# A GNN message layer on one core: a new opening order, clears and loads in smaller and larger pieces, and second operands of VectorE in PSUM

## The chip, the cores and the metric

The kernel runs on one core of one Trainium2 chip. The metric is the time of the device in microseconds (us). Five engines matter: PE multiplies matrices, DVE (VectorE) and ACT (ScalarE) work on elements, POOL (GpSimd) here issues the indirect DMAs, SP (SyncE) issues most other DMAs. Each engine takes its own instructions in a fixed order and waits on semaphores for the others.

## The reference, cut to what matters

```python
# x (6250, 128), src and dst (100000,), edge_attr (100000, 128), W (384, 128); dst is sorted
row, col = src, dst
h = concatenate([x[row], x[col], edge_attr], -1) @ W + b
h = (h - mean(h)) * rsqrt(var(h) + 1e-5) * gamma + beta      # over the 128 features
out = segment_sum(relu(h), row, num_segments=6250)
y = x + out
return (y - mean(y)) / sqrt(var(y) + 1e-5)
```

Every edge gets a message from its two nodes and its own features, the messages are normalized, and each node sums the messages of the edges that have it as `src`. The edges come sorted by `dst`, so the sum needs another order.

## The kernel before, in words

The weight matrix is split into three: `xa = x @ W[0]` (with the bias) for the source node, `xb = x @ W[1]` for the target node and `eT @ W[2]` for the edge. Means are taken out of the weights beforehand.

Edges are worked on in 782 tiles of 128, four tiles to a piece; there are 196 pieces, and one call of `edges` handles one of them (a slot). Because `dst` is sorted, a piece needs only 42 neighbouring rows of `xb`: `win` loads that window from the table `xb_d` in DRAM (three bf16 parts), `db` loads the piece's offsets within the window for all partitions (from `drel_d`), DVE makes the one-hot `ohd` from it (L345), and PE adds `eT @ W[2]` (L351) and `ohd @ win` (L352) in the PSUM tile `hp`. ACT copies it to one of eight buffers `hs` (L354) with the local node number beside it (L356), and POOL scatters the rows, one indirect DMA for each tile (L360), to the DRAM table `sorted` of the split, where the edges of one block of nodes stand together.

Where a row goes is worked out by `places` for a group of tiles: a one-hot over the 50 blocks (`oh`, L264), a running count (`sc`, L266, a scan over 50 x T elements), products (`far` L280, `sc` L281), sixteen matmuls (L287), and small instructions that end in `place_i` (L305).

The tiles are in three splits of 260, 260 and 262 tiles, each with its own `sorted` table. While the edges of split s + 1 are scattered, the 50 blocks of split s are worked on: `begin` loads a block (`hl`, L411, 6 x 128 rows), makes the one-hot `ohe` of local node numbers (L415) and transposes it (`tr` L422, `ohn` L423); `middle` adds the gathered `xa` rows to `hl` in PSUM (`sel`, L433 and L437), squares and sums (ACT, L441), and makes `msg` (DVE, L449); `end` sums the messages of each node (`pa`, L457) into `acc`. The blocks of split 2 have no edges beside them. `finish` (L467) handles five blocks' worth of nodes at the very end: residual and layer norm.

Before the first `edges` call stand the set-up of constants and weights, `source_blocks` (block and local number of each source), `windows` (the offsets, written to `drel_d`), thirteen projections `project(g, 1)` that write `xb_d`, and the first group of places. Rows of `sorted` that no edge fills are cleared by three large DMAs on ACT's queue (`clear`, L147). `side` holds the other groups of places, two other small steps, the projections `project(g, 0)` that make `xa`, and the other clears; one of them is given out in every second slot of split 0.

The order on each engine is the work of a scheduler with priorities, from the order of the calls and from buffers; only the opening stands under a higher priority. PSUM has eight banks: two `hp`, one `pa`, two `tr`, three `sel`.

Of the kernel before, what the change touches and what calls it, by code (L numbers as in the profile page):

```python
# [15 lines left out]
P = 128  # L16
# [7 lines left out]
NB, BN = 50, 125  # L24
NPAD = 6400
PT = 4
WN = 42
PIECES = 196
# [3 lines left out]
SPLITS = [(260, 6, 4, [32, 66, 66, 66, 30]), (260, 6, 4, [65] * 4), (262, 6, 4, [66, 66, 66, 64])]  # L32
TMAX = 66
PG = 7
G = 3
# [32 lines left out]
def fast_path(ctx, tc, io, bad_d):  # L68
# [9 lines left out]
    xb_d = dram.tile([3, NPAD, D], BF16, name="xb_d")  # L78
# [10 lines left out]
    proj_pool = early.enter_context(tc.tile_pool(name="proj", bufs=2))  # L89
    src_i = setup.tile([P, TILES], I32, name="src_i")  # L90
    nc.sync.dma_start(src_i, io["srcT"])
    dst_i = setup.tile([HALF, 2, PT * P], I32, name="dst_i")
    nc.sync.dma_start(dst_i, io["dstC"])
    w3 = const.tile([P, 3, D], F32, name="w3")
    nc.scalar.dma_start(w3, io["W"].rearrange("(k p) d -> p k d", p=P))
    base_i = const.tile([1, PIECES], I32, name="base_i")
    nc.scalar.dma_start(base_i, io["base"])
# [3 lines left out]
    for t, v in ((gamma_bc, io["gamma"]), (b_bc, io["b"]), (beta_bc, io["beta"])):  # L101
        nc.scalar.dma_start(t, dram_ap(v, 0, [[0, P], [1, D]]))
# [4 lines left out]
    nc.gpsimd.iota(part_i, pattern=[[1, 1]], base=0, channel_multiplier=1)  # L107
    spare_i = setup.tile([P, TMAX], I32, name="spare_i")
    nc.gpsimd.iota(spare_i, pattern=[[P, TMAX]], base=0, channel_multiplier=1)
    ident = const.tile([P, P], F32, name="ident")  # L110
    make_identity(nc, ident)
    eps = const.tile([P, 1], F32, name="eps")
    nc.vector.memset(eps, LN_EPS)
    iota_row = const.tile([P, P], F32, name="iota_row")
    nc.vector.tensor_copy(iota_row, iota_i)
    iota_h = const.tile([P, NB], BF16, name="iota_h")
    nc.vector.tensor_copy(iota_h, iota_i[:, :NB])
    part = const.tile([P, 1], F32, name="part")
    nc.vector.tensor_copy(part, part_i)
    ones_h = const.tile([P, P], BF16, name="ones_h")  # L120
    nc.vector.memset(ones_h, 1.0)
# [16 lines left out]

    spare_rows = max(k - f for _, k, f, _ in SPLITS)
    empty = const.tile([P, spare_rows, ROW], F32, name="empty")  # L140
# [3 lines left out]
    def clear(s):  # L144
        _, k, f, _ = SPLITS[s]
        per = k - f
        return nc.scalar.dma_start(  # L147
            dram_ap(sorted_d[s], f * P * ROW, [[per * ROW, P], [k * P * ROW, NB], [1, per * ROW]]),
            row_bc(flat(empty[:, :per, :]), NB))
# [4 lines left out]
    nc.vector.tensor_scalar(sgn, gamma_bc, 0.0, 2.0, op0=ALU.is_ge, op1=ALU.mult)  # L154
    nc.vector.tensor_scalar(sgn, sgn, -1.0, None, op0=ALU.add)
    wsum = const.tile([P, 4], F32, name="wsum")
    nc.vector.tensor_reduce(wsum[:, 0:3], w3, axis=AX.X, op=ALU.add)
    nc.vector.tensor_reduce(wsum[:, 3:4], b_bc.unsqueeze(1), axis=AX.X, op=ALU.add)
    wmean = const.tile([P, 4], F32, name="wmean")
    nc.vector.tensor_scalar(wmean, wsum, 1.0 / D, None, op0=ALU.mult)  # L160
    w = const.tile([P, 3, D], F32, name="w")
    for j in (1, 2, 0):
        nc.vector.scalar_tensor_tensor(w[:, j, :], w3[:, j, :], wmean[:, j:j + 1], sgn,
                                       op0=ALU.subtract, op1=ALU.mult)
    bias = const.tile([P, D], F32, name="bias")
    nc.vector.scalar_tensor_tensor(bias, b_bc, wmean[:, 3:4], sgn, op0=ALU.subtract, op1=ALU.mult)
# [7 lines left out]
    def source_blocks(t0, t1):  # L174
# [7 lines left out]
        nc.vector.tensor_copy(bkt_h[:, c], bkt[:, c])  # L182
        if t1 == TILES:
            for p0 in range(LAST, P, 32):
                nc.vector.memset(bkt_h[p0:p0 + 32, TILES - 1:TILES], 99.0)


    bad = const.tile([P, 3], F32, name="bad")
# [23 lines left out]


    xa = tabs.tile([P, NB, 3 * D], BF16, name="xa")
    acc = tabs.tile([P, NB, ACW], F32, name="acc")
    XG = 4
    n_proj = -(-NB // XG)

    def project(g, k):

        t0 = g * XG
        m = min(XG, NB - t0)
        xT = proj_pool.tile([P, XG * P], F32, name="xT", bufs=4)
        nc.sync.dma_start(xT[:, :m * P], io["xT"][:, t0 * P:(t0 + m) * P])
        ps = psum.tile([P, 4, P], F32, name="hp", bufs=2)
        for j in range(m):
            nc.tensor.matmul(ps[:, j, :], xT[:, j * P:(j + 1) * P], w[:, k, :],
                             start=True, stop=True)
        full = ps[:, :m, :]
        if k == 0:  # L230
            o = xa[:, t0:t0 + m, :]
# [3 lines left out]
        else:  # L235
            xb_t = proj_pool.tile([P, XG, 3 * D], BF16, name="xb")
            o = xb_t[:, :m, :]
        nc.scalar.copy(o[:, :, 0:D], full)
        rest_t = proj_pool.tile([P, XG, D], F32, name="rest")
        rest = rest_t[:, :m, :]  # L240
        nc.vector.tensor_tensor(rest, full, o[:, :, 0:D], op=ALU.subtract)
        nc.scalar.copy(o[:, :, D:2 * D], rest)
        nc.vector.tensor_tensor(o[:, :, 2 * D:3 * D], rest, o[:, :, D:2 * D], op=ALU.subtract)
        if k == 1:
            for i in range(3):
                nc.sync.dma_start(
                    dram_ap(xb_d, i * NPAD * D + t0 * D, [[NB * D, P], [D, m], [1, D]]),
                    o[:, :, i * D:(i + 1) * D])
# [7 lines left out]
    def places(s, t0, T):  # L256
        cap = SPLITS[s][1] * P
# [5 lines left out]
            for t in (oh, sc, far)]  # L263
        nc.vector.tensor_tensor(oh_v, row_bc(bkt_h[:, t0:t0 + T], NB), col_bc(iota_h, T),  # L264
                                op=ALU.is_equal)
        nc.vector.tensor_tensor_scan(flat(sc_v), flat(oh_v), flat(oh_v), 0.0,  # L266
# [9 lines left out]
        at = place_pool.tile([P, NB], F32, name="at")  # L276
# [49 lines left out]
    def edges(s, q):  # L326
# [28 lines left out]
        with tc.issue_after(evict.ins):  # L355
            nc.scalar.copy(hs[:, :m, D], sloc[:, t0:t0 + m])  # L356
# [463 lines left out]
```

## Time and profile before

| | before |
|---|---|
| time, median of 3 runs | 1531.3 us (1529.97 to 1536.56) |
| time of the profiled execution | 1529.89 us |
| its span in the profile | 1528.1 us |
| granted TensorE clock, mean of the span | 0.874 |
| PE / DVE / ACT / POOL busy | 1162.9 / 805.0 / 658.8 / 843.7 us |
| DMA packets, bytes, mean rate | 147179, 238.46 MB, 156 GB/s |

The span is the profiled part of one execution; 1.8 us of its time lie around it. Busy time is the sum of the instructions' durations; an engine can be idle for long and still set the end, and a busy one can be off the path. In a row of a group, the numbers after the first bar are busy time and the mean ns of one instruction, those after the second the idle time before them and what ended it. In the slices each digit is the busy share of a fortieth of the span (38.2 us) in tenths.

### The profile page before, as it was taken

How to read it: one execution, taken by the hardware profiler on the slowest of the kernel's cores; microseconds unless marked ns; L12 is line 12 of the kernel's file. 1: busy time of each engine (PE TensorE's matmuls, PEld its weight loads, DVE VectorE, ACT ScalarE, POOL GpSimd, SP SyncE). 2: the span in 40 equal slices, each digit the busy share in tenths (PEclk: the TensorE clock that was granted, in tenths of full speed). 3: DMA queues.
4: the chain of work that ended last, by engine and by line, in shares of the span. 5: the costliest groups of instructions: out<-in, count | busy, mean ns of one | idle time of the engine just before them, and what ended most of it. 6: DMA issues, size and time to landing. Idle time of an engine off the chain costs nothing.

```text
span 1528.1 us, 26702 instructions
## 1 busy us (share of the span) xinstructions
PE 1162.9 (76%) x8886; PEld 948.1 (62%) x8886; DVE 805.0 (53%) x2127; ACT 658.8 (43%) x2706; POOL 843.7 (55%) x804
## 2 busy tenths in 40 slices
PE   2555565564565479999999839999999848888885
PEld 2233444353343348888888728888888637677674
DVE  6999453432313425445544305545545327777766
ACT  0011212121010026766666516666676526666563
POOL 0000787877878877777777777777777720000000
PEclk9687877765667679999999959999999969999998
DMA  9944534443333346766666447676767223333330
GB/s 322 347 106 104 168 127 136 134 143 113 118 127 111 103 139 208 207 204 205 202 201 198 127 143 226 204 217 196 211 198 204 74 91 99 101 101 94 109 92 31
DMA packets 147179, 238.46 MB, mean 156 GB/s; under 512 B 64050, under 2 KB 84291, under 8 KB 147031
## 3 DMA queue, kind: packets, MB, share of 16 engines
q1 hardware_dynamic: 101924, 163.14, 37.4%
q0 software_dynamic: 25024, 52.85, 9.7%
q10 hardware_dynamic: 20082, 20.67, 4.3%
q8 instruction: 72, 1.18, 0.3%
q14 instruction: 77, 0.62, 0.1%
HBM read 155.11 MB, written 81.47 MB: 155 GB/s over the span
## 4 chain that ended last, share of the span: by engine, by line
PE 46%; POOL 16%; DVE 14%; DMA 12%; issue 9%; ACT 2%; SPq 0%; ACTq 0%; POOLq 0%; DVEq 0%
POOL sorted L360 16%; PE pa L457 11%; PE sel L433 11%; DMA sorted<-hs,place_i 10%; PE sel L437 8%; PE hp L351 7%; PE tr L422 6%; DVE sc L266 2%; DVE ohe L415 2%; PE pa L287 2%; PE hp L352 2%; DVE msg L449 1%; DVE far L280 1%; ACT sq L441 1%; DVE y L477 1%
## 5 line engine op out<-in xcount | busy, mean ns | idle before, releaser
L360 POOL DMA_INDIRECT sorted<-hs,place_i x782 | 841.9, 1077 | 392.8 <-issue 192.4
L351 PE MATMUL hp<-w,eT 128*128 128x128 f32 x1564 | 324.1, 333 | 171.6 <-ACT hs L354 164.8
L351 PEld LDWEIGHTS hp<-w,eT 128*128 128x128 f32 x1564 | 273.7, 219 | 217.0 <-ACT hs L354 189.9
L354 ACT COPY hs<-hp 128x512 f32<-128x512 f32 x196 | 114.7, 585 | 508.3 <-DMA sorted<-hs,place_i 353.0
L441 ACT ACTIVATE sq<-sel 128x128 f32<-128x128 f32 x900 | 251.7, 280 | 128.0 <-PE sel L437 101.8
L433 PE MATMUL sel<-hl,ident 128*128 128x384 f32 x600 | 260.6, 517 | 24.6 <-DVE frstd L484 15.2
L449 DVE SCALAR_TENSOR_TENSOR msg<-sel,rstd,cut 128x128 f32<-128x128 f32 x900 | 247.4, 342 | 1.5
L457 PE MATMUL pa<-msg,ohe 128*128 128x130 f32 x1800 | 244.7, 282 | 2.4 <-DVE msg L449 1.3
L437 PEld LDWEIGHTS <-ohn 128*128 128x128 bf16 x2700 | 182.2, 98 | 92.5 <-issue 58.2
L457 PEld LDWEIGHTS pa<-msg,ohe 128*128 128x128 f32 x1800 | 220.3, 192 | 8.3 <-DVE msg L449 4.8
L437 PE MATMUL sel<-xa,ohn 128*128 128x128 bf16 x2700 | 211.0, 220 | 0.0
L352 PE MATMUL hp<-win,ohd 126*128 126x128 bf16 x782 | 186.0, 239 | 26.0 <-DVE ohd L345 24.4
L441 ACT ACTIVATION_READ_ACCUMULATOR sq<-sel 128x1 f32 x900 | 176.7, 196 | 0.0
L415 DVE TENSOR_TENSOR ohe<-hl,iota_row 128x768 f32<-128x768 f32 x150 | 140.7, 939 | 66.3 <-DMA hl<-sorted 66.3
L423 ACT CAST ohn<-tr 128x384 bf16<-128x384 f32 x300 | 129.3, 482 | 76.0 <-PE tr L422 73.8
L422 PE MATMUL tr<-ident,ohe 128*128 128x128 f32 x900 | 127.7, 279 | 40.5 <-DVE bad_t L565 27.3
L345 DVE TENSOR_SCALAR ohd<-db,part_w 128x512 bf16<-128x512 bf16 x196 | 67.9, 358 | 161.3 <-PE hp L352 141.1
L422 PEld LDWEIGHTS tr<-ident,ohe 128*128 128x128 f32 x900 | 102.0, 144 | 59.1 <-DVE bad_t L565 27.4
L446 DVE RECIPROCAL rstd<-std 128x6 f32<-128x6 f32 x150 | 28.2, 188 | 194.6 <-ACT std L444 193.4
L433 PEld LDWEIGHTS sel<-hl,ident 128*128 128x128 f32 x600 | 92.4, 194 | 29.3 <-issue 17.1
L352 PEld LDWEIGHTS <-ohd 126*128 126x128 bf16 x782 | 85.8, 110 | 28.4 <-DVE ohd L345 25.8
L287 PE MATMUL pa<-far,ident 128*128 128x462 f32 (+4 forms) x208 | 94.6, 593 | 6.9 <-DVE far L280 6.0
(116 smaller groups left out, 692.6 us busy)
## 6 DMA issues: line engine op xcount, KB each, us to landing
hl<-sorted SPq DMA_DIRECT2D x150, 396.0 KB
eT<-in_eT SPq DMA_DIRECT2D x97, 512.0 KB
db<-drel_d SPq DMA_DIRECT2D x98, 256.0 KB
sorted<-empty ACTq DMA_DIRECT2D x3, 6600.0 KB
sorted<-hs,place_i POOLq DMA_INDIRECT x782
win<-xb_d SPq DMA_DIRECT2D x196, 31.5 KB
xT<-in_xT SPq DMA_DIRECT2D x24, 256.0 KB
xb_d<-xb SPq DMA_DIRECT2D x36, 128.0 KB
```

The costliest lines, as they stand in the source:

```text
L287: nc.tensor.matmul(sums[:, :g * T], wt, flat(v[:, b:b + g, :]), start=(k == 0 and b == 0), stop=(k == 1 and b + PG >= NB), skip_group_chec ...
L351: nc.tensor.matmul(hp[:, j, :], eT[:, at], w[:, 2, :], start=True, stop=False)
L352: nc.tensor.matmul(hp[:, j, :], oh[:3 * WN, at], win[:3 * WN, :], start=False, stop=True)
L360: i = nc.gpsimd.indirect_dma_start(out=sorted_d[s][:, :], out_offset=bass.IndirectOffsetOnAxis(ap=place_i[:parts, t:t + 1], axis=0), in_=h ...
L415: nc.vector.tensor_tensor(self.ohe[:, :k, :], self.hl[:, :k, D:D + 1].to_broadcast([P, k, P]), row_bc(iota_row, k), op=ALU.is_equal)
L422: nc.tensor.transpose(tr[:, j, :], self.ohe[:, j0 + j, :], ident)
L423: nc.scalar.copy(self.ohn[:, j0:j0 + m, :], tr[:, :m, :])
L433: nc.tensor.matmul(sel[:, :m, :], ident, self.hl[:, j0:j0 + m, 0:D], start=True, stop=False)
L437: nc.tensor.matmul(sel[:, j, :], self.ohn[:, j0 + j, :], xa[:, self.b, i * D:(i + 1) * D], start=False, stop=(j == m - 1 and i == 2))
L441: nc.scalar.activation(sq, sel[:, j, :], AF.Square, accum_out=ss[:, j0 + j:j0 + j + 1])
L449: nc.vector.scalar_tensor_tensor(self.msg[:, j0 + j, 0:D], sel[:, j, :], rstd[:, j0 + j:j0 + j + 1], cut, op0=ALU.mult, op1=ALU.max)
L457: nc.tensor.matmul(pa[:, :ACW], self.ohe[:, j, :], self.msg[:, j, :], start=(j == 0), stop=(j == k - 1))
```

## The change

1. The opening is written out by hand: PE, DVE, ACT and SP take split 0's instructions in the order of the calls (`manual_schedule`), up to the end of split 0. The first group of places has 16 tiles, then 48, 65, 65, 66. Inputs are loaded in pieces; `places` and `project` are cut into steps (`yield`; `project_a`, `project_b`) that are given out slot by slot, places of splits 0 and 1 in split 0 and those of split 2 in split 1.
2. `xb` goes to two tables in node order: 1024 rows (the first two projections, for pieces 0 to 27) and the rest. Window starts are clamped to their table (`bases`), and a check is added.
3. `clear` writes a pair of blocks at a time, in runs of eight rows. Split 0's clears are five DMAs on POOL's queue; those of splits 1 and 2 are 25 each on SP's queue, one in a slot, behind that slot's window.
4. `hl` is loaded for two blocks at once, whose rows alternate in `sorted`, in two buffers; `bkt` and `place` are worked out for that layout. `eT` and `db` are loaded for three pieces in two buffers (two pieces in three before). Loads, windows and `ohd` are issued four, three and two slots ahead.
5. One PSUM bank, `beside`, holds the row 0..127, a zero and `at`. It is the second operand of `oh`, of the scan, of `far` and of `ohe`. For this `sel` has two banks where it had three; in the blocks of split 2 the second `sel` of a block takes a bank of `hp`.

```diff
-SPLITS = [(260, 6, 4, [32, 66, 66, 66, 30]), (260, 6, 4, [65] * 4), (262, 6, 4, [66, 66, 66, 64])]
+SPLITS = [(260, 6, 4, [16, 48, 65, 65, 66]), (260, 6, 4, [65] * 4), (262, 6, 4, [65, 65, 66, 66])]
...
+    beside = psum.tile([P, 512], F32, name="beside")
+    iota_p, zero_p, at = beside[:, 0:P], beside[:, P:P + 1], beside[:, 2 * P:2 * P + NB]
...
-    def clear(s):
+    def clear(s, p0, n, queue):
         _, k, f, _ = SPLITS[s]
-        per = k - f
-        return nc.scalar.dma_start(
-            dram_ap(sorted_d[s], f * P * ROW, [[per * ROW, P], [k * P * ROW, NB], [1, per * ROW]]),
-            row_bc(flat(empty[:, :per, :]), NB))
+        parts = 2 * (k - f) * P // RUN
+        return queue.dma_start(
+            dram_ap(sorted_d[s], (p0 * k + f) * 2 * P * ROW,
+                    [[RUN * ROW, parts], [2 * k * P * ROW, n], [1, RUN * ROW]]),
+            row_bc(flat(empty[:parts, :, :]), n))
...
-        nc.vector.tensor_tensor(oh_v, row_bc(bkt_h[:, t0:t0 + T], NB), col_bc(iota_h, T),
-                                op=ALU.is_equal)
-        nc.vector.tensor_tensor_scan(flat(sc_v), flat(oh_v), flat(oh_v), 0.0,
+        nc.vector.tensor_tensor(oh_v, row_bc(bkt_h[:, t0:t0 + T], NB),
+                                col_bc(iota_p[:, :NB], T), op=ALU.is_equal)
+        nc.vector.tensor_tensor_scan(flat(sc_v), flat(oh_v),
+                                     zero_p.to_broadcast([P, NB * T]), 0.0,
                                      op0=ALU.add, op1=ALU.max)
...
-        at = place_pool.tile([P, NB], F32, name="at")
+        yield
         nc.vector.tensor_tensor(at, room[s], ps[:, 0:NB], op=ALU.add)
...
         nc.vector.tensor_tensor(far_v, oh_v, col_bc(at, T), op=ALU.mult)
         nc.vector.tensor_tensor(sc_v, sc_v, oh_v, op=ALU.mult)
+        yield
...
-    HS, DG = 8, 2
+    HS, DG = 8, 3
...
+    def edge_loads(q):
+        if q % DG or q >= PIECES:
+            return
...
+        eT = edge.tile([P, DG * PT * P], F32, name="eT", bufs=2)
...
+        db = edge.tile([P, DG * PT * P], BF16, name="db", bufs=2)
...
+    def edge_window(q):
...
+        win = edge.tile([P, D], BF16, name="win", bufs=6)
+        i = nc.sync.dma_start(win[:3 * WN, :], xb_d[k][:, bass.ds(base, WN), :])
+        held["win", q] = win
+        return i
+
+    def edge_hot(q):
...
+        nc.vector.tensor_scalar(oh[:, :m * P], held[q // DG][1][:, c0:c0 + m * P], part_w, None,
+                                op0=ALU.is_equal)
...
-            self.hl = blk.tile([P, KMAX, ROW], F32, name="hl", bufs=4)
-            nc.sync.dma_start(
-                flat(self.hl[:, :k, :]),
-                dram_ap(sorted_d[self.s], self.b * k * P * ROW, [[k * ROW, P], [1, k * ROW]]))
+            if self.b % 2 == 0:
+                pair = blk.tile([P, 2 * KMAX, ROW], F32, name="hl", bufs=2)
+                nc.sync.dma_start(
+                    flat(pair[:, :2 * k, :]),
+                    dram_ap(sorted_d[self.s], self.b * k * P * ROW,
+                            [[2 * k * ROW, P], [1, 2 * k * ROW]]))
+                late["pair"] = pair
+            pair = late["pair"]
+            self.hl = bass.AP(tensor=pair.tensor, offset=pair.offset + self.b % 2 * ROW,
+                              ap=[list(pair.ap[0]), [2 * ROW, k], [1, ROW]])
...
-                                    self.hl[:, :k, D:D + 1].to_broadcast([P, k, P]),
-                                    row_bc(iota_row, k), op=ALU.is_equal)
+                                    self.hl[:, :, D:D + 1].to_broadcast([P, k, P]),
+                                    row_bc(iota_p, k), op=ALU.is_equal)
...
-                sel = psum.tile([P, G, P], F32, name="sel", bufs=3)
+                sel_t = psum.tile([P, PT, P], F32, name="hp" if at_end and j0 else "sel", bufs=2)
+                sel = sel_t[:, :G, :]
...
+    first = places(0, 0, n0)
+    order = ExitStack()
+    order.enter_context(tc.manual_schedule(engines={
+        mybir.EngineType.PE, mybir.EngineType.DVE, mybir.EngineType.Activation,
+        mybir.EngineType.SP}))
+    for p0 in range(0, NB // 2, 5):
+        clear(0, p0, 5, nc.gpsimd)
+    source_blocks(0, n0)
+    signs()
+    weights(1, 2)
+    project_a(0, 1)
+    run(first)
+    load_x(2, 1)
+    load_x(3, 1)
+    windows()
+    edge_loads(0)
+    project_b(0, 1)
+    project_a(1, 1)
+    run(first, 2)
+    bases()
+    project_b(1, 1)
+    weights(2, 3)
+    run(first, 2)
+    for q in range(3):
+        edge_window(q)
+    edge_loads(3)
+    edge_hot(0)
+    edge_hot(1)
+    source_blocks(n0, TILES)
+    weights(0, 1)
+    biases()
...
         for i in range(slots):
-            edges(s, p0 + i)
-            n_work = -(-len(work) // (slots - i)) if s else (1 if i % 2 == 0 or len(work) >= slots - i else 0)
-            for _ in range(min(n_work, len(work))):
+            q = p0 + i
+            edge_loads(q + 4)
+            w_in = edge_window(q + 3)
+            edge_hot(q + 2)
+            edges(s, q)
+            if s + 1 < n_split and 5 <= i < 5 + NB // 2:
+                with tc.issue_after(w_in.ins):
+                    clear(s + 1, i - 5, 1, nc.sync)
+            want = min(n_work, max(min(urgent, i + 1), (i + 1) * n_work // (slots - 4)))
+            for _ in range(want - done_work):
                 work.pop(0)()
-            if s == 0 and not work and not late:
+            done_work = want
+            if s == 0:
+                want = min(n_x, 2 * (i + 1))
+                for _ in range(want - done_x):
+                    side_x.pop(0)()
+                done_x = want
+            if s == 0 and not side_x and not late:
                 open_late()
...
+        if s == 0:
+            order.close()
```

In the changed kernel the lines of `places` are L330 (`oh`), L332 (the scan), L347 (`far`), L348 (`sc`), L355 (its matmuls), those of `edges` L442, L443, L445 and L452, and those of a block L504, L513, L533, L549 and L557.

## The prediction

> **What bounds the kernel now.** I read the page's slices first, then one table of windows, one window per stage, then the timeline where GpSimd's scatters are slow, then the chain of the last stage. A slot is one call of `edges` (four tiles, four scatters); a block is 125 nodes of one split.
>
> ```profile
> PE   2555565564565479999999839999999848888885
> DVE  6999453432313425445544305545545327777766
> POOL 0000787877878877777777777777777720000000
> DMA  9944534443333346766666447676767223333330
> ```
> POOL, which issues the 782 scatters, does nothing in the first four slices (38 us each) and in the last seven. Nothing that makes a scatter possible is ready before 157 us.
>
> ```profile
> L360 POOL DMA_INDIRECT sorted<-hs,place_i x782 | 841.9, 1077 | 392.8 <-issue 192.4 <-ACT hs L356 155.6 <-DMA sorted<-hs,place_i 22.6
> ```
> ```profile
> 157.00:549.00 392.00, 219.97 (x1089) 165.93 (x1087) 143.22 (x204) 61.31 (x166) 314.44 (x255) 0.71 0.41 127
> 549.00:862.00 313.00, 299.44 (x2603) 255.31 (x2604) 155.52 (x498) 197.58 (x833) 240.73 (x238) 0.97 0.67 198
> 862.00:1237.00 375.00, 323.97 (x2881) 280.95 (x2879) 163.53 (x532) 217.32 (x919) 286.60 (x291) 0.93 0.59 177
> 1242.00:1516.00 274.00, 240.51 (x2016) 194.40 (x2016) 194.83 (x668) 165.31 (x760) 0.00 (x0) 0.97 0.30 93
> ```
> The first line is the scatter's group on the page; the others are windows (length; busy us and count of PE, PEld, DVE, ACT, POOL; granted clock; DMA share; GB/s). Between scatters POOL waits 0.30 us for nothing shown, and an undisturbed one takes 0.96 us. So 1.262 us each, 5.05 us a slot, 987 us for all 782 is the floor. From 157 to 1237 they took 1080: 93 over the floor, of which split 0 (392 us for 65 slots, 6.03 each) holds most. In splits 1 and 2, PE is 86 to 96% busy beside POOL.
>
> ```profile
> 153.27 6.93 DVE L266 TENSOR_TENSOR_SCAN sc<-oh 128x3250 bf16<-128x3250 bf16 x1
> 157.12 4.01 POOL L360 DMA_INDIRECT sorted<-hs,place_i  x1 [154.67 <-ACT hs L356]
> 160.98 1.85 DVE L281 TENSOR_TENSOR sc<-sc,oh 128x3250 bf16<-128x3250 bf16 x1
> 161.44 2.22 POOL L360 DMA_INDIRECT sorted<-hs,place_i  x1 [0.30 <-issue]
> 163.96 0.96 POOL L360 DMA_INDIRECT sorted<-hs,place_i  x1 [0.31 <-issue]
> ```
> A scatter that starts inside a DVE instruction with two SBUF tensors ends 0.9 us after that instruction. Going through the timeline from 150 to 620 us, the excess over 0.96 us beside L266 is 33.7 us (6 scatters), beside L280 15.1 (6), beside L264 14.3 (5), beside L281 7.1 (6): 11 us per group of places from the first three, 1.2 from L281.
>
> ```profile
> 1296.48 0.29 DVE L462 TENSOR_TENSOR acc<-acc,pa 128x130 f32<-128x130 f32 x1 [2.02 <-PE pa L457]
> 1301.21 0.29 DVE L462 TENSOR_TENSOR acc<-acc,pa 128x130 f32<-128x130 f32 x1 [1.80 <-PE pa L457]
> ```
> ```profile
> 1276.67 1.55 DVE msg L449 x6
> 1303.17 1.55 DVE msg L449 x6
> ```
> ```profile
> PE sel L433 <- DVE frstd L484: 15.2, 9, 1.7
> ```
> The last stage: first two lines of DVE's timeline (one block is 4.73 us, and DVE waits for PE in it), then two lines of the chain (the pattern repeats every 26.5 us, five blocks and one `finish`), then a line of the waits. So a `finish` adds 26.5 - 5 x 4.73 = 2.85 us: its DVE work delays `msg`, so the third `sel` buffer, so PE.
>
> **The change part by part.** The sum is for the profiled execution: span 1528.1, time 1529.9 (1.8 around the span); the median shown is 1.4 above it.
>
> Opening. Before, the first scatter stands at 157. The window of the first 50 us shows DMA share 1.01 at 328 GB/s. The new opening must move the 6.8 MB clear of split 0, the first inputs and projections (src, dst, four xT, w, broadcasts, drel, eT, db, three xb_d writes: 4.8 MB): 11.6 MB at 328 GB/s is 35 us, from 2.5 us on, and 2 to 3 us for window, matmul, eviction: **first scatter at 40 us**. DVE's written order up to the first place_i is some 55 instructions of 0.06 to 0.95 us and one scan of 1.75 (half the 1600-element one, 3.48): 22 us, hidden. SP issues drel, eT, db, xb_d, windows in order; drel's round trip took 7.2 + 7.7 us before. The five clears now stand ahead of the scatters on POOL's queue. The nearest row is the scatter: 128 rows in 0.96 us, so 320 rows 2.4 us, 12 in all, hidden below 40. By bytes instead (20 times a scatter's) 19 us each: a first scatter near 100. I take the rows; the other end is in the range. Below: 30.
>
> Slot pace in split 0. DVE, PE, ACT and SP now run in written order. The rest of `source_blocks` (766 columns, ten to twelve instructions of 0.5 to 0.9 us) and the 48-tile places stand in front of slot 4: DVE is at 28 with db, +8.5, then places 8 + 5, then PE's sixteen matmuls (8 to 9 us), then pos: about 67, where POOL would be at 60. From slot 9 the 65-tile groups put 10.5 us of DVE (L264 + L266) and 11 us of PE (L287 at the low clock) into a slot, with both `hp` buffers shared with the projections and no lead built up yet: about 12 us more near slots 14 to 16. Stalls: **22 us** (5 to 60). Later eight `hs` buffers (40 us) cover them. On SP an xb_d write waits for DVE's last difference with the next slot's window and loads queued behind it; they now go three and four slots ahead (15 to 20 us), ohd two on DVE, which covers that wait once there is a lead. DVE in split 0: 8 groups at about 18 us, 24 projections at 1.4 to 2.1, 65 ohd at 0.36: 215 us of 328, not the bound.
>
> Locks. In the new order nearly all twelve groups fall beside scatters (six did). L264, L266 and L280 get one operand in PSUM. Durations: the same rows (3.54, 6.94, 3.54), since 3250 elements in 3.54 us already show no faster mode. What is left: L281 with two SBUF inputs (12 x 1.2 = 14 us), the projections' differences (6), ohd (10: of the 93, some 72 are in that list; the other 20 I share between ohd and ohe, and ohe now reads PSUM): 30 us. The skill's "SBUF — State Buffer", section "Who interferes with whom", says that such a `tensor_tensor` contends only with GpSimd's reads, and infers that it doesn't stall descriptor generation, which needs the write interface. By that rule the PSUM operands are worth nothing. The trace's 33.7 + 15.1 + 14.3 us decide against that inference: with eleven groups beside scatters, keeping the old operands would cost 11 x 11 = 120 us here. The same section says that at most one SBUF input outside the two-port modes doesn't contend; no row of before has a large DVE op with PSUM beside scatters (`msg`, 1.64 us, is the nearest: scatters beside it stay at 0.96). I use that.
>
> POOL's end: 40 + 987 + 30 + 22 = **1079** (was 1237).
>
> Splits 1 and 2. `sel` has two buffers where it had three, so PE's next `sel` waits for `msg`: after the last `sel` of a block come 1.4 (sq), 0.3 (std), 0.2 (rstd), 0.85 (three msg) and handovers, 3.0 us. The changed order puts 12 edge matmuls (1.5 slots, 2.0 us), tr and pa into it, 3 us before the wait: covered. PE's 4.5 + 2.0 = 6.5 us per block stays below POOL's 1.5 x 5.05 = 7.6. Pair loads: hl goes from 150 loads to 75 of 792 KB, two buffers; the next may start when both blocks have been read. One 396 KB load came in 3.1 us (issue 1238.3, first reader 1241.4); 792 KB: 4.4 us (estimate, 1.2 more at 340 GB/s). The loop is L + 4.1 us (ohe, msg, two sel) per two blocks, against 15.2: L may reach 11. SP's 50 later clears (270 KB) are issued behind windows, in slots at 60 to 75% DMA share: nothing, with L as the price. eT/db come three slots at a time, the same six slots of buffer. The places of split 2 stay in split 1 and read the same rows.
>
> The lag behind POOL. This costs. With 1.5 slots per block, PE has issued the last edges when 84 blocks are done; 16 blocks of split 1 remain, without edges to cover the two-buffer wait: 2.3 + 0.3 + 3.0 + 0.3 = 5.9 us each, 94 us. PE is eight to nine slots (44 us) ahead of POOL: **50 us** after POOL's end, where before the first block of the last split began 5 us after it.
>
> Last stage. Four banks (two sel, two free hp). Per five blocks DVE needs 5 x 3.05 + 7.4 = 22.6 us, PE 23.0 (87% of 26.5). Between these and 26.5 I take 24.5: 245 us for 50 blocks, was 273. The end after the last pa (1515 to 1528): 13.
>
> Costed at nothing: base clamping, the two checks, the doubled place formula (same count of instructions), 39 xb_d writes becoming 14. They stand beside POOL's time; on DVE they'd be under 5 us.
>
> Sum: 1079 + 50 + 245 + 13 = 1387, +1.8: 1389; **1388**.
>
> **Rivals.**
> Stalled opening (17%): the written order and 1.4 to 1.6 MB a slot (4.6 to 5.4 us at 300 to 350 GB/s) keep POOL waiting through the first 25 slots, or the clears are priced by bytes. For: DMA 9 in the first slices, PE clock 0.6 to 0.8. 25 slots at 7.5: +60, 1448.
> Better than thought (14%): no stall, last stage at PE's own 23.0 and a lag of 35: 1388 - 22 - 15 - 15 = 1336.
> The PSUM operand doesn't free POOL (6%): +120, 1508: most of the gain is eaten.
> Slower (7%): pair loads set the pace of splits 1 and 2. SP sends one behind eT and db (1.2 MB) and a waiting issue, L = 15 us: (15 + 4.1) / 2 = 9.55 us per block instead of 7.6, 87 blocks' worth of slots: +170, 1558. It decides above L = 11 and turns the gain into a loss above about 14.4. For: drel and db needed 7 us in the saturated opening, and the load can't start before the second block is read. Against: the share is 0.6 to 0.7 there, and 396 KB came in 3.1.
> Forecast (56%).
>
> **Numbers.** 0.5% (8 us) is about what a measurement of this kernel tells from no change. Faster: the forecast, the first two rivals and a third of the PSUM case: 0.89. The PSUM case with small errors elsewhere gives the rest: same 0.03, slower 0.08 with the last rival. Its range leaves out the slower and the PSUM case and small parts of the tails: 1336 to 1450.
>
> **What would show it.** POOL's digits begin in slice 2; first scatter 30 to 55 us; no scatter of 4 to 7 us beside the scan, some of 2 beside L348; slot pace 5.1 in splits 1 and 2; POOL's last scatter at 1050 to 1110; then PE still at split 1's blocks for 35 to 65 us with waits of sel for msg; last stage 23 to 26 us per five blocks. Wrong if scatters stay long beside L332, if hl's landings rule DVE's waits, or if POOL idles in split 0.

## The result, and the profile after

The changed kernel takes 1442.9 us (median of 4 runs, 1442.6 to 1443.7), beside 1532.1 for the kernel before on the same chip (1530.0 to 1536.6): a ratio of 0.9415, 95% interval 0.9393 to 0.9437. The forecast was 1388 with 1336 to 1450, so the time lies in the range, 55 us above its middle. The experiments then met other chips, on one of which the same change makes the kernel 2.3% slower. Both results need an explanation.

First the slices of the page and its row of scatters (slices are 36 us here).

```profile
PE   2364475656565989979979999999887799899895
DVE  4637557555731475484474445444444457877776
POOL 1265556777777777777777777777775000000000
DMA  9477644534456777555556566656533223323330
...
L452 POOL DMA_INDIRECT sorted<-hs,place_i x782 | 763.1, 976 | 338.0 <-issue 195.2
```

POOL now starts in the second slice instead of the fifth. Its busy time fell from 841.9 to 763.1 us, and a scatter's mean from 1077 to 976 ns: the long scatters are gone (the longest is 2.52 us, beside L348). But POOL's digits are 5 and 6 in slices 3 to 7 where they should be 7, and PE still needs nine slices after POOL's end.

Next, the changed kernel by stage (window; length; busy us and count of PE, PEld, DVE, ACT, POOL; granted clock; DMA share; GB/s): opening, the three splits of scatters, the time from the last scatter to the first finished block of the last split, the last stage.

```profile
0.00:50.00 50.00, 10.54 (x54) 9.31 (x54) 23.75 (x82) 4.37 (x7) 5.99 (x27) 0.75 0.85 235
50.00:442.00 392.00, 226.74 (x1262) 179.40 (x1262) 229.66 (x309) 75.03 (x189) 256.77 (x259) 0.76 0.55 172
442.00:775.00 333.00, 298.04 (x2428) 249.08 (x2429) 183.80 (x474) 176.25 (x732) 253.46 (x261) 0.94 0.65 205
775.00:1108.00 333.00, 311.38 (x2699) 264.56 (x2697) 153.19 (x499) 200.22 (x857) 252.88 (x263) 0.99 0.56 186
1108.00:1183.00 75.00, 61.14 (x534) 49.54 (x535) 37.76 (x120) 43.69 (x196) 0.00 (x0) 1.00 0.24 77
1183.00:1429.00 246.00, 223.51 (x1916) 185.01 (x1915) 187.72 (x647) 156.32 (x727) 0.00 (x0) 0.97 0.29 97
```

The opening has two parts, by the same columns:

```profile
2.50:43.00 40.50, 8.35 (x44) 7.63 (x45) 16.73 (x60) 3.69 (x5) 4.13 (x18) 0.78 0.99 278
43.00:50.20 7.20, 2.19 (x10) 1.68 (x9) 6.76 (x17) 0.68 (x2) 0.00 (x0) 0.50 0.27 66
```

Up to 43 us the DMA engines are full, at 278 GB/s (the kernel before moved 341 in the same stretch). Then they are nearly idle for 7.2 us: the first windows land 3 us after their issue, the first slot's matmuls run at half the clock, and ACT copies.

In splits 1 and 2 POOL is at its floor: 253 us busy in 333, which, with the 0.30 us between scatters, is all that it can do. In split 0 it is not. The fifth line is 75 us in which POOL has nothing left and the blocks of split 1 are still being worked off; before, this stretch was 19 us.

Where POOL stands still in split 0, the timeline reads like this (DVE, PE and POOL of the changed kernel).

```profile
167.83 3.54 DVE L330 TENSOR_TENSOR oh<-bkt_h,beside 128x3250 bf16<-128x3250 bf16 x1
171.40 6.92 DVE L332 TENSOR_TENSOR_SCAN sc<-oh,beside 128x3250 bf16<-128x3250 bf16 x1
174.28 0.96 POOL L452 DMA_INDIRECT sorted<-hs,place_i  x1 [0.30 <-issue]
178.59 0.21 DVE L339 TENSOR_TENSOR cnt<-end 128x50 bf16<-128x50 f32 x1
178.86 0.20 PE L341 MATMUL pa<-cnt,before 128*128 128x50 bf16 x1 [13.46 <-DVE cnt L339]
184.63 0.96 POOL L452 DMA_INDIRECT sorted<-hs,place_i  x1 [9.38 <-ACT hs L448]
```

A scatter that starts inside the scan keeps its 0.96 us: the lock, by which DVE's instruction held it, is gone. But in the written order PE's small matmul L341 stands in front of the next slot's edges and waits 13.46 us for `cnt`, so POOL runs dry for 9.38. Eleven holes of 1 to 10 us between 65 and 235, this among them, add up to 56 us beyond the usual 0.30 each.

At the end PE is well ahead of POOL with the edges, and behind with the blocks. Its last edge matmul, and the last scatter:

```profile
1072.05 0.22 PE L443 MATMUL hp<-win,ohd 126*128 126x128 bf16 x1
1106.91 0.87 POOL L452 DMA_INDIRECT sorted<-hs,place_i  x1 [0.31 <-issue]
```

PE is done with the edges 35.5 us before POOL, and 18 blocks of split 1 still lack their `acc` at that moment (3 before the change). After the last scatter, a block of split 1 comes every 5.94 us, with DVE waiting 3.00 us for PE in each:

```profile
1119.52 0.29 DVE L562 TENSOR_TENSOR acc<-acc,pa 128x130 f32<-128x130 f32 x1 [3.00 <-PE pa L557]
1125.45 0.29 DVE L562 TENSOR_TENSOR acc<-acc,pa 128x130 f32<-128x130 f32 x1 [3.00 <-PE pa L557]
```

**The budget.** In the table, each stage's length is read from the timelines: first scatter; the splits by the 260th, 520th and last scatter; "lag" from the last scatter to block 101's `acc`; "last stage" from there to block 150's. The last two rows tell of PE's last edge matmul: how long before POOL's last scatter it ends, and how many blocks of split 1 have no `acc` yet. The first two columns are the chip of the prediction. The next two are both kernels unaltered on the two chips of most experiments, where before takes 1804 and 1801 us (c2_before_again and c1_after_again, below). The last two are two versions with a third `sel` buffer (e8, e10, below); e8 belongs with the second pair, e10 with the first.

| us | before | after | before (c2) | after (c1) | e8 | e10 |
|---|---|---|---|---|---|---|
| first scatter | 157.1 | 50.2 | 157.3 | 49.8 | 49.8 | 51.8 |
| split 0 | 397.3 | 392.1 | 434.0 | 432.5 | 430.3 | 375.9 |
| split 1 | 342.8 | 332.5 | 457.9 | 519.1 | 509.8 | 362.1 |
| split 2 | 339.9 | 333.0 | 459.3 | 472.9 | 470.3 | 332.3 |
| lag | 18.7 | 75.0 | 17.0 | 107.4 | 16.3 | 18.0 |
| last stage | 259.3 | 245.8 | 259.4 | 245.7 | 235.3 | 235.4 |
| span | 1528.1 | 1441.6 | 1797.6 | 1840.1 | 1724.5 | 1388.3 |
| PE ahead of POOL | 30.5 | 35.5 | 2.9 | 3.2 | 3.4 | 25.3 |
| blocks left (count) | 3 | 18 | 3 | 18 | 4 | 3 |

On the first chip the change brings 107 us at the opening, 22 in the splits and 13 in the last stage, and gives 56 back in the lag: -86.5.

### The profile page after: what moved, and what is told of

Read it like the earlier page. It is cut to its first block, busy times and chain, and to the rows that moved or that the text cites. A ratio compares the mean times of both kernels' runs of the same rounds, so it can differ in the third digit from the quotient of the medians.

```text
span 1441.6 us, 26396 instructions
## 1 busy us (share of the span) xinstructions
PE 1131.3 (78%) x8890; PEld 936.9 (65%) x8890; DVE 821.9 (57%) x2150; ACT 656.2 (46%) x2706; POOL 769.1 (53%) x809
## 4 chain that ended last, share of the span: by engine, by line
PE 56%; DVE 16%; DMA 11%; issue 7%; POOL 6%; ACT 3%; SPq 0%; ACTq 0%; DVEq 0%; POOLq 0%
PE pa L557 13%; PE sel L533 10%; PE sel L537 8%; PE hp L442 7%; PE tr L520 6%; POOL sorted L452 6%; PE pa L355 5%; DMA sorted<-hs,place_i 5%; DVE sc L332 3%; PE hp L533 3%; DMA db<-drel_d 2%; DMA eT<-in_eT 2%; DVE oh L330 2%; PE hp L537 2%; PE hp L443 2%
## 5 line engine op out<-in xcount | busy, mean ns | idle before, releaser
L452 POOL DMA_INDIRECT sorted<-hs,place_i x782 | 763.1, 976 | 338.0 <-issue 195.2
L442 PE MATMUL hp<-w,eT 128*128 128x128 f32 x1564 | 319.9, 327 | 55.5 <-ACT hs L445 32.4
L442 PEld LDWEIGHTS hp<-w,eT 128*128 128x128 f32 x1564 | 265.4, 213 | 89.4 <-ACT hs L445 38.2
L541 ACT ACTIVATE sq<-sel 128x128 f32<-128x128 f32 x750 | 208.0, 277 | 185.4 <-PE sel L537 159.6
L557 PE MATMUL pa<-msg,ohe 128*128 128x130 f32 x1800 | 264.0, 284 | 17.1 <-DVE msg L549 16.9
L445 ACT COPY hs<-hp 128x512 f32<-128x512 f32 x196 | 113.8, 580 | 310.3 <-issue 152.1
L557 PEld LDWEIGHTS pa<-msg,ohe 128*128 128x128 f32 x1800 | 230.5, 194 | 25.5 <-DVE msg L549 18.1
L533 PE MATMUL sel<-hl,ident 128*128 128x384 f32 x500 | 215.7, 514 | 18.8 <-issue 10.4
L549 DVE SCALAR_TENSOR_TENSOR msg<-sel,rstd,cut 128x128 f32<-128x128 f32 x750 | 207.6, 343 | 3.1
L443 PE MATMUL hp<-win,ohd 126*128 126x128 bf16 x782 | 182.0, 234 | 29.4 <-DMA win<-xb_d 22.0
L537 PE MATMUL sel<-xa,ohn 128*128 128x128 bf16 x2250 | 169.3, 221 | 0.0
L541 ACT ACTIVATION_READ_ACCUMULATOR sq<-sel 128x1 f32 x750 | 146.2, 195 | 0.0
L513 DVE TENSOR_TENSOR ohe<-hl,beside 128x768 f32<-128x768 f32 x150 | 141.8, 946 | 0.0
L562 DVE TENSOR_TENSOR acc<-acc,pa 128x130 f32<-128x130 f32 x100 | 28.4, 284 | 186.9 <-PE pa L557 186.9
L443 PEld LDWEIGHTS <-ohd 126*128 126x128 bf16 x782 | 83.4, 107 | 18.0 <-DVE ohd L428 17.9
L533 PEld LDWEIGHTS sel<-hl,ident 128*128 128x128 f32 x500 | 78.6, 198 | 21.2 <-issue 21.2
L560 DVE COPY acc<-pa 128x130 f32<-128x130 f32 x50 | 14.3, 285 | 130.7 <-PE pa L557 130.7
```

Of the source, the lines that this page charges most:

```text
L442: nc.tensor.matmul(hp[:, j, :], eT[:, at], w[:, 2, :], start=True, stop=False)
L443: nc.tensor.matmul(hp[:, j, :], oh[:3 * WN, at], win[:3 * WN, :], start=False, stop=True)
L445: evict = nc.scalar.copy(hs[:, :m, 0:D], hp[:, :m, :])
L452: i = nc.gpsimd.indirect_dma_start(out=sorted_d[s][:, :], out_offset=bass.IndirectOffsetOnAxis(ap=place_i[:parts, t:t + 1], axis=0), in_=h ...
L513: nc.vector.tensor_tensor(self.ohe[:, :k, :], self.hl[:, :, D:D + 1].to_broadcast([P, k, P]), row_bc(iota_p, k), op=ALU.is_equal)
L533: nc.tensor.matmul(sel[:, :m, :], ident, self.hl[:, j0:j0 + m, 0:D], start=True, stop=False)
```

## The experiments

Twelve kernels ran. Eleven fell on two chips on which the kernel before takes 1801 and 1804 us, the last on one where it takes 1531. So each is told by its ratio to the kernel before on its own chip, and its stages are read from its own trace.

**The changed kernel again (c1_after_again), unaltered; the control of what follows.** 

> The changed kernel unaltered, on the same chip as the next three. It should repeat the ratio 0.94 to before and the trace's marks: first scatter at 50, scatter mean 976 ns, last scatter at 1107, block 101 at 1183. On a chip where before takes longer than 1532 us, all theories give the ratio another value; the three that follow are then read against this run.

Measured: 1841.6 us, ratio 1.0228 (1.0201 to 1.0255); the 0.94 did not repeat. The first scatter, the scatter mean (971 ns) and the last stage repeat; splits 1 and 2 take 327 us more than in the first trace. The chain of the page names what the first trace doesn't have at all:

```profile
PE 45%; another core or an unknown queue 18%; DVE 16%; issue 13%; ACT 4%; DMA 3%; SPq 0%; ACTq 0%; DVEq 0%
```

And these are its windows for splits 1 and 2:

```profile
482.00:1001.00 519.00, 347.94 (x2407) 281.48 (x2408) 186.20 (x468) 172.65 (x713) 249.53 (x260) 0.80 0.43 135
1001.00:1474.00 473.00, 348.17 (x2576) 289.31 (x2576) 145.72 (x473) 191.23 (x799) 251.99 (x264) 0.83 0.40 130
```

The granted clock is 0.80 and 0.83 where it was 0.94 and 0.99. POOL's busy time is the same, in half as much time again. In the timeline ACT and DVE stand for 10 us and more without a releaser on this core (`remote`), while PE's matmuls that they need are recorded as done:

```profile
1022.45 1.11 PE L557 MATMUL pa<-msg,ohe 128*128 128x130 f32 x8
1027.48 0.96 POOL L452 DMA_INDIRECT sorted<-hs,place_i  x1 [0.30 <-issue]
1030.55 0.29 DVE L560 COPY acc<-pa 128x130 f32<-128x130 f32 x1 [10.07 <-remote]
```

POOL issues at its usual pace until it runs dry; DVE gets `pa` 7 us after PE's record of it ends. So on this chip PE's results come late and PE is the bound, not POOL: its last edge matmul ends only 3.2 us before the last scatter, where it was 35.5. Around this wait the granted clock falls to half:

```profile
1016.00:1027.00 11.00, 9.68 (x85) 8.34 (x82) 3.30 (x11) 4.79 (x21) 6.53 (x7) 1.00 0.37 119
1028.00:1034.00 6.00, 2.24 (x11) 2.17 (x12) 3.11 (x10) 2.93 (x11) 1.40 (x2) 0.50 0.42 128
```

At each of the 45 waits of this kind over 5 us in splits 1 and 2 it stands at 0.50 within 2 us of the wait's end. Counted in windows of 1 us, the clock is below 0.75 for 366 of the 992 us of these splits here, and for 43 of 666 in the first trace, which has no such wait. An estimate from these counts: half the clock in 323 us more costs PE at most half of them, some 160 of the 327 us lost. Ends of matmuls are modelled in the profile, so the trace doesn't tell whether the low clock is the cause of the waits or goes with them; the rest of the loss, and why this chip does so, stay open. What its other cores did meanwhile isn't on record.

**The kernel before again (c2_before_again), unaltered, for its trace.** 

> The kernel before unaltered, for its trace on the chip on which the changed kernel takes 1842 us. If the chip takes from both kernels by the same cause, the splits after the first show DVE's waits for acc of about 10 us with no releaser and a granted clock of 0.80 to 0.88 as the changed kernel does there, and its last stage takes the same as in the first trace (259 us from block 101 to block 150). If the cause is the changed kernel's own, these waits are rare here and the time is lost elsewhere.

1800.0 us. It loses its time in the same place: splits 1 and 2 take 917 us instead of 683 (granted clock 0.89 and 0.90), the last stage 259.4 instead of 259.3. Waits of `acc` without a releaser are fewer, though (34 us in all beside the changed kernel's 274); with all other instructions of DVE and ACT such waits come to 447 us beside 615, and the clock is below 0.75 for 194 of the 917 us. So such a chip slows both, and the changed kernel more. The table says where, as far as two chips that agree within 0.2% on before can be set side by side: 107 us are won at the opening and 14 in the last stage, 61 are lost in split 1, 14 in split 2 and 90 in the lag. The lag is settled below; what costs 52 us in split 1 even in e8, without the lag, stays open.

**The SBUF operands back (e1_sbuf_operands).** The bank stays reserved. In short:

```
-  ... col_bc(iota_p[:, :NB], T)     / zero_p.to_broadcast(...)  / at in PSUM / row_bc(iota_p, k)
+  ... col_bc(iota_h, T)             / flat(oh_v)                / at in SBUF / row_bc(iota_row, k)
```


> The changed kernel with DVE's second operands back in SBUF (iota, the scan's second input, the places' base, the blocks' one-hot); the bank stays reserved, so sel keeps two buffers and all else is as after. If the operand in PSUM is what keeps POOL free, scatters beside the scan, the one-hot and the product take 4 to 7 us again, about 11 us for each group of places that falls on running scatters: the scatter group's mean goes from 976 ns to 1050 to 1110, POOL's end moves by 50 to 110 us, time 1495 to 1550. If an SBUF tensor_tensor only contends for reads and doesn't stall the descriptors, the time stays at 1443 within 8 us.

1857.1 us, ratio 1.0323 (1.0247 to 1.0399), beside 1.0228 for the control; the two intervals overlap. Its row of scatters, and the scatters beside one group of places:

```profile
L453 POOL DMA_INDIRECT sorted<-hs,place_i x782 | 879.7, 1125 | 633.4 <-ACT hs L449 374.3
```
```profile
116.26 3.54 DVE L331 TENSOR_TENSOR oh<-bkt_h,iota_h 128x3250 bf16<-128x3250 bf16 x1
116.47 4.15 POOL L453 DMA_INDIRECT sorted<-hs,place_i  x1 [0.31 <-issue]
119.83 6.93 DVE L333 TENSOR_TENSOR_SCAN sc<-oh 128x3250 bf16<-128x3250 bf16 x1
120.93 6.59 POOL L453 DMA_INDIRECT sorted<-hs,place_i  x1 [0.30 <-issue]
```

The long scatters are back, one in each DVE instruction, each ending about 0.8 us after it. POOL's busy time is 120.0 us above the control's 759.7: the forecast's 11 groups at 11 us. What scatters take over 0.96 us is 55.8 us beside the scan, 34.2 beside `oh` and 32.0 beside `far`. This is the place where the inference of the Trainium skill ("SBUF — State Buffer", "Who interferes with whom") about descriptor generation would have given nothing; it doesn't hold for these scatters. But the time moved by 1% where some 50 to 110 us were expected: POOL waited for 708 us in the control anyway, its end came 45 us later, and the lag became 35 shorter. Most of the shorter lag is no effect of the lock: the scheduler's order came out otherwise here, 1.36 slots of edges to a block (1.48 in the control) and 13 blocks left after PE's last edges (18), so this pair doesn't give the lock's worth in time; e8 and e2 below do.

**SBUF operands, and their bank to `sel` (e2_sbuf_three_sel).** The edit of e1, without the reserved bank, and `bufs=3` for `sel`. 

> As the kernel with SBUF operands, and the bank that they left goes to sel as a third buffer, as before. Told by the difference to that kernel. If the two buffers are what makes the lag behind POOL's last scatter, the blocks of split 1 that are left then take about 5.0 us each where they take 5.9, and more of them are done before: 15 to 40 us less. If the lag comes from the order in which the edges' matmuls are put ahead of the blocks, the number of blocks left stays at about 13 and the difference is 10 to 15 us.

1771.6 us, ratio 0.9827 (0.9751 to 0.9903): 4.8% below e1, some 85 us. The lag falls from 73 to 18 us. Both theories named something true: the bank decides it, and it does so through the order. With three buffers the trace has 1.20 slots of edges to a block up to block 45 and 3 blocks without `acc` after the last edges, both as before the change; with two, e1 has 1.36 and 13, the changed kernel 1.48 and 18.

**The PSUM operands alone (e3_before_psum).** The kernel before with the four operands in PSUM, and `bufs=2` for `sel`. 

> The kernel before with only the PSUM operands, which take the bank of sel's third buffer. If the operands free POOL: scatter mean from 1077 to about 1000 ns, POOL's end 45 to 60 us earlier (1177 to 1192); two sel buffers without the free banks of the changed kernel's last stage then cost 20 to 30 us there and 20 to 40 of lag: time 1520 to 1550, so about nothing or a small loss. If the operands are worth nothing, POOL's end stays at 1237 and the time is 1570 to 1600.

1954.7 us, ratio 1.0882 (1.0799 to 1.0964). The scatters fall to 974 ns and POOL is 81 us less busy, but its end is only 8 us earlier (1500.4, beside c2's 1508.5), the lag is 127 us and the last stage 310. Read against c2, the bank costs 161 us where the operands gain 8. The trace agrees: 1.50 slots to a block, and 21 blocks left. I had put 40 to 70 for the bank and 45 to 60 for the operands; that POOL's end moved so little fits PE being the bound on this chip (3.1 us ahead of POOL at the end). The other misses are the lag (110 us more than before, expected 20 to 40) and the last stage (51 more, expected 20 to 30).

**The written order kept to the end (e4_written_all).**

```
-        if s == 0:
+        if s == n_split - 1:
             order.close()
```


> The changed kernel with the written order of PE, DVE, ACT and SP kept to the end of the third split, not to the end of the first. Blocks then stay where the loop writes them, 50 over 60 slots, and no edges can be taken ahead of them. If the scheduler's order makes the lag, block 101's accumulation comes 15 to 30 us after POOL's last scatter where it comes 75 after: 1390 to 1405. If two sel buffers alone make the lag, or the written order stalls PE by more than it saves, the time is 1435 or above.

2116.8 us, ratio 1.1766 (1.1687 to 1.1845). The lag is 23 us as I expected, but POOL's end moves from 1474 to 1830. A line of its waits:

```profile
DVE rstd L546 <- ACT std L544: 707.0, 118, 12.3
```

In the written order a block's `rstd` waits for ACT's `std` with the edges' `ohd` and the next block's one-hot queued behind it on DVE. The lag goes, and the price is far above it.

**SP's opening in another order (e5_drel_first).**

```
-    load_x(2, 1); load_x(3, 1); windows(); edge_loads(0); project_b(0, 1)
+    windows(); project_b(0, 1)
...
+    edge_loads(0)          # after project_b(1, 1), db ahead of eT
+    load_x(2, 1); load_x(3, 1); src_i rest
```


> SP's opening in another order: the drel write goes out ahead of two xT loads and the rest of src, the two xb_d writes ahead of the wait for drel, db ahead of eT. If the queue order is what put the first scatter at 50 us, it comes at 36 to 42 and the time is 8 to 14 us less. If the transfers themselves fill the opening (12.3 MB in the first 50 us), it comes at 47 to 52 and the time is the same within 5 us.

1841.6 us, ratio 1.0233 (1.0209 to 1.0258), as the control. The first scatter came at 54.6, not at 36 to 42: db was issued 3 us earlier, but took 20 us to land instead of 12. So this order of the queue doesn't bring the first scatter forward.

**The small matmuls one step later (e6_counts_later).** `yield` moved from behind the two matmuls with `cnt` to in front of them. 

> The two small matmuls that follow DVE's cnt are written one step of places later, so PE no longer stands before cnt with the next slot's edges behind it. If that wait is what stalls POOL in split 0, its idle time between 50 and 250 us goes from about 57 to 20 to 35 us and the time is 20 to 35 us less. If the stalls come from PE's and DVE's work as such at the low clock, they stay within 10 us and so does the time.

1828.3 us, ratio 1.0164 (1.0138 to 1.0190): 0.6% or 12 us below the control. POOL's waits between the first scatter and 250 us fall from 66 to 56. The wait for `cnt` is part of the stalls, but not most of them: the expectation of 20 to 35 us was wrong.

**The edges held back (e7_held_edges).**

```
-            edges(s, q)
+            if s > 0 and len(ended) >= 4:
+                with tc.issue_after(ended[-4].last.ins):   # last matmul of that block's pa
+                    edges(s, q)
+            else:
+                edges(s, q)
```


> In splits 1 and 2 PE's edge matmuls are queued behind the end of the fourth block back, so the scheduler puts about 1.2 slots of edges to a block where it put 1.5, and 5 blocks of split 1 are left after the last edges where 16 were. If the order makes the lag, block 101 comes 20 to 45 us after the last scatter instead of 75 and the time is 30 to 55 us less. If PE is full in these splits anyway, the last scatter comes later by what the lag loses and the time is the same within 10 us.

1788.7 us, ratio 0.9927 (0.9898 to 0.9955): 53 us below the control. The lag is 35.8 instead of 107.4 us; the last scatter came 21 us later. It left 6 blocks after the last edges, with two buffers. So the order alone makes most of the lag, and some of what it saves is PE's work that has to be done earlier.

**PSUM operands in spare columns (e8_spare_columns).** In short:

```
-    beside = psum.tile([P, 512], F32, name="beside")
+    trs = [psum.tile([P, 512], F32, name=f"tr{i}") for i in range(2)]   # 384 columns for transposes
+    iota_p, zero_p, at = trs[0][:, 384:], trs[1][:, 384:385], trs[1][:, 448:498]
...
+    sel: bufs=3
```


> The changed kernel with its PSUM operands kept in the spare columns of the two banks of tr (a block's transposes fill 384 of 512), so they take no bank, and sel has three buffers again. If the bank is what the PSUM operands cost, the edges stand again at 1.2 slots to a block, block 101 follows 20 to 40 us after the last scatter, the scatter mean stays at 970 ns, and the time is 80 to 110 us below the changed kernel's 1842 on this chip: 1730 to 1765. If the loss on this chip comes from anything else in the change, the time stays above 1800. If reading a bank that PE writes holds DVE up, ohe and the places' one-hot get longer than 0.95 and 3.55 us.

1728.9 us, ratio 0.9598 (0.9522 to 0.9674). Against the control's 1.0228 that is 6% or 113 us, a little more than expected. The scatter mean is 971 ns, `ohe` 939, so these columns serve DVE as well as a bank of their own. PE's transposes ran during only 4 of the 189 reads by `ohe`, `oh`, the scan and `far`, though; what reads and writes of one bank at the same time would cost, this trace hardly shows. The lag is 16.3, the last stage 235.3. Against e2, which differs in where the operands lie and has the same 1.20 slots to a block, it is 2.3% (intervals don't touch): here the lock is worth about 41 us, with POOL's end 43 us earlier.

**The same with the two later edits (e9_spare_later).** 

> As the kernel with the operands in tr's spare columns, with the two later edits as well: the places' small matmuls one step later, and the edges held behind the fourth block back. The first takes 10 to 20 us out of split 0 as it did alone; the second should do nothing where the edges already stand at 1.2 slots to a block. 10 to 20 us below the spare columns alone; if both act on PE's order alone and PE is full, the same within 5.

1719.1 us, ratio 0.9538 (0.9470 to 0.9606): 10 us below e8, within its interval. Split 0 is 9 us shorter, as in e6.

**Clears on ACT's queue (e10_clears_act).** e8 with e6's edit, and `clear(0, p0, 5, nc.scalar)` instead of `nc.gpsimd`. 

> The kernel with the operands in tr's spare columns and the later counts, and the five clears of split 0 issued by ACT's queue instead of GpSimd's. In the changed kernel's first 50 us the clears' 6.76 MB took 52.1% of 16 engines' time, 16 GB/s for each engine, where the clears of before on ACT's queue moved 20 GB/s for each. If it is GpSimd's queue that makes them slow, the first scatter comes at 38 to 44 us and the time is 6 to 12 us below the 1719 of its neighbour. If it is the shape of the clears (4 KB pieces, into every second block pair) or the reads that share the opening, it stays at 48 to 52 and the time at 1719 within 6.

This one ran on a chip where before takes 1531.5 us: 1390.7, ratio 0.9091 (0.9061 to 0.9121). The neighbour with 1719 us isn't comparable; the changed kernel's 0.9415 is, and this is 3.4% less. Of the edit itself, the first scatter is the answer: 51.8 us. The clears' 7.15 MB (with ACT's other loads) took 58.3% of 16 engines' 50 us, 15 GB/s for each, as on GpSimd's queue. So it isn't the queue; the shape of the clears and the loads beside them weren't told apart. The rest of the gain is that of e8 and e6, and here it can be read in the slices:

```profile
PE   2466575556565999989989999999999859999995
...
POOL 0365566777777777775656777777777720000000
```

Split 0 is 16 us shorter than in the changed kernel, the lag 57, the last stage 10. Split 1 is 30 longer: PE does 2755 matmuls there where the changed kernel did 2428 and left the rest for after POOL's end. It beats both kernels; e8 and e9, its near relatives, beat before by 4 and 5% where before takes 1804 us.

## Why the prediction was right, and where it was off

The direction and the range held; the sum missed by 55 us. By its own steps:

- **First scatter, 40; measured 50.2.** The amount was right (11.6 MB forecast, 12.3 MB moved in the first 52 us), two other terms were not. While the DMA engines are full, this opening runs at 278 GB/s, not at before's 328, so they are full until 43 us. And window, matmul and eviction took 7.2 us at half the clock, not 2 to 3. Neither another order on SP (54.6) nor another queue for the clears (51.8) changed the sum, and why the rate is lower stays open. The price of the clears on POOL's queue by rows was right, too high even: 3.57 us for all five, where I took 12.
- **Stalls in split 0, 22; measured 56.** Inside the bounds I gave (5 to 60). I counted DVE's and PE's work in front of a slot, but not that a small matmul in a written order waits for a long DVE instruction with edges queued behind it. That accounts for about a sixth (66 to 56 in e6); how the rest divides between PE's sixteen place matmuls and the low clock (0.76) wasn't told apart.
- **Locks, 30; measured about 12** (763.1 less 782 times 0.96), 10 of them beside L348; the 10 that I gave to `ohd` came to 0.2. The step that spoke against the inference held, and e1 gave the 120 us that I had worked out for the old operands in the new order. What I missed is that those microseconds count only where POOL is the bound.
- **POOL's end, 1079; measured 1107.8**, the sum of these three. Splits 1 and 2 at POOL's floor: right on this chip (5.1 us a slot).
- **The lag.** Mechanism right, term mis-sized. I worked out 16 blocks at 5.9 us, less a lead of PE of 44 us, to the start of the last split's blocks. Before, that start lay 13.8 us ahead of block 101's `acc`; put there after the change, it gives 61 us where I had 50. The blocks took 5.94 each, and 16 had not begun when PE's last edges were done: right. The lead was 35.5 us, and that is 8.5 of the 11. I gave the lag to the two buffers and the order as two causes; e2, e7 and e8 show that the buffers set the order.
- **The last stage, 24.5 us for five blocks; measured 24.8 and 26.5 in turn.** "Four banks" was too kind: only a block's second `sel` took the free banks, its first still shared two. DVE's 22.6 us for five blocks was put too high, too: in before's 26.5 us it is busy for 19.7. With the third `sel` buffer (e8, e10) it is 24.5.

Summed: +29 at POOL's end, +11 for the lag, +15 for the last stage (measured against before's marks), together the 55.

**The rivals.** The stalled opening (1448) came nearest in number and in place: half the miss is first scatter and split 0. The PSUM rival is refuted by e1 and e8. The slower case was to come from the pair loads; in the changed kernel's trace `ohe` never waits for `hl`. That the time fell in the range owes something to luck: a first scatter 10 us late and 34 us more of stalls were in part made up by locks 18 us cheaper. Slower did occur, on another chip, by none of the cases I had: with PE late in splits 1 and 2, the opening's gain doesn't reach the end, and the lag grows to 107. The sum holds where POOL is the bound of the splits, and I wrote down PE's 86 to 96% there without asking what a later PE would make of the change.

## What to carry to other kernels

A PSUM bank spent on a constant is paid in the pipeline that loses the buffer, and through the scheduler's order it can be paid far from there; look first for spare columns in a bank that is in use, and at what else touches that bank at the same time, which these runs hardly show. When an engine is freed, ask which one is next at 90%: here a gain of 107 us at the front became 86 on one chip and a loss on another, because PE stood that close behind POOL. In an order written by hand, put a matmul that waits for a long instruction behind the work that doesn't.

## What the runs showed of the hardware

- A scatter issued by GpSimd inside a DVE instruction with two SBUF tensors lasts until 0.8 us or so after that instruction (4.15 and 6.59 us beside 3.54 and 6.93); with one operand in PSUM it keeps 0.96, but for three beside `oh` of up to 1.41. What is left is L348, with two SBUF inputs: up to 2.52 us.
- DVE reads the spare columns of a bank that PE's transposes write as fast as a bank of their own: 939 ns for `ohe`, beside 946. The two ran at the same time in only 4 of 189 reads.
- The same program takes 1443 us on one chip and 1842 on another. The granted clock in the splits is 0.94 to 0.99 on the first and 0.80 to 0.83 on the second, the last stage is the same to 0.1 us, and the second shows waits for PE's results of 10 us and more that the first has none of, each with the clock at 0.50. A verdict from one chip didn't carry to the next: 0.94 became 1.02.
- Clears in pieces of 4 KB (with ACT's loads, in one case) moved 15 to 16 GB/s for each DMA engine on either queue; before's, in packets of 1 KB and with other loads beside them, 20. What makes the difference was not tested.
